# The last layer's first pair of tiles made among the last output products, block sums issued later, and three tiles for the weights' finer sums

## The chip, the cores and the metric

The kernel runs on one core of a Trainium2 chip. Its time is the device time in microseconds (us) of one execution. PE is TensorE (matmuls and transposes), DVE is VectorE, ACT is ScalarE, POOL is GpSimd, and SP is SyncE, whose only work here is to issue DMAs, in order. L1015 is line 1015 of the kernel before.

## The reference, cut to what matters

Four layers act on x, 8 batches of 256 rows by 1024 columns, all in float32. Each layer adds its result, times a gate, to x.

```python
x = x + g0 * autocorrelation(x, ctx)          # through a Fourier transform
x = x + g1 * lora_ffn(norm(x))                # 1024 x 1024 weight with a low-rank part
q, k, v = norm(x) @ wq, ctx @ wk, ctx @ wv    # 32 query heads, 8 key/value groups of 4 heads
x = x + g2 * softmax(mask(rope(q) @ rope(k).T)) @ v @ wo
x = x + g3 * (norm(x) @ w1 + b1)              # the "Fourier" layer; w1 is made on the chip
```

## The kernel before

The batches are done in two passes of four, `p = 0` and `p = 1`. A pass keeps its x as eight tiles of 128 rows by 1024 columns (`xt`), in two blocks `blk` of four tiles. It runs its four layers one after the other: `autocorrelation` with `keys_values` beside it, `lora_ffn`, `attention`, `fourier_ffn`.

The large products are Strassen products: a product of 2 by 2 blocks is made of seven block products (`SEVEN`, in the order 1, 2, 6, 7, 4, 5, 3) on sums of blocks. `left_operands` makes the sums of a left side with four additions or subtractions, and what a product gives is added to x at once by `add_product` (L261 to L275, with the scaled addition `residual`, L381).

**Attention** takes 16 steps (blk, group). A step has four rounds `i`. In each round it issues the `scores` of one batch and head pair (L1142), some of the next step's `queries` (L985), the softmax on ACT and DVE (L1151 to L1165), and the `values` (transposes at L1177, products at L1188). Outputs, the products with `wo`, are generators: `o_gen` is advanced by so many yields at each place (`o_fill`, `fill_from`), so that PE has work while a softmax is under way.

- In pass 0 `outputs` makes the 7 products of one step (L1015, 14 matmul groups of 128x512). `load_wo` brings its seven weight tiles. In the odd steps of block 1 (steps 9, 11, 13 and 15) `finer_weights` also makes, for each of the seven weights, four more half tiles for pass 1: two subtractions on DVE (L931, L932), two on POOL (L933, L934) into the tiles `t67` and `t45`, and a store of each to `wo2_d` (L935, L936). Each of `t67` and `t45` has one buffer, and the generator gives one of the seven per round.
- In pass 1 (`paired`) `outputs_of_two` makes the outputs of two steps at once, with 7 x 7 = 49 products (L1078). POOL makes the finer left operands (`oI`, L1061), DVE combines the quarters (L1086 to L1098), and DVE and POOL add them to x (L1105). The weights come through `stream_wo`: 28 tiles of 4 KB per partition for a pair of steps (four for each of the seven outer products: one in two DMAs of 256 KB, two of 512 KB, one of 256 KB), each issued seven tiles ahead of its use.

When the last step's `values` are issued, the outputs of the last step (p = 0) or the last pair of steps (p = 1) follow with nothing between them. Then `fourier_ffn` begins. It takes its tiles in four pairs. `prepare` takes the norm's statistics of four tiles at once (`norm_stats`: L359, L360), normalises a tile into `xn` (L366, DVE), transposes it on PE (L376, eight transposes per tile) and copies it out of PSUM (L377, ACT). `left` then makes the sums of a pair, and `project` its seven products (L1327, four matmuls each). The next pair is prepared ahead of the products of a pair.

**What decides the order.** The code is written for a tile framework: a scheduler orders each engine's instructions by its own estimates of their times, with the order of the source as priority, and puts in the waits. Buffers come from pools. The two large groups "a" and "b" have seven buffers of 4 KB per partition each (`big_tile`); in a pass, `gq` holds the query weights and later the Fourier weights, and `go` holds the output weights `wo`. A tile that asks for a buffer waits until the earlier one in its slot has no more readers.

Of the kernel before, what the change touches and what calls it, by code (L numbers as in the profile page):

```python
# [11 lines left out]
F32 = mybir.dt.float32  # L12
# [7 lines left out]
P = 128  # L20
# [26 lines left out]
def flamingo_kernel(ctx: ExitStack, tc: tile.TileContext, a: dict, out: bass.AP):  # L47
# [303 lines left out]
    def norm_stats(tiles):  # L351

        n = len(tiles)
        mv = stats.tile([P, TT, 2], F32, tag="mv", name="mv")
        rstd = stats.tile([P, TT], F32, tag="rstd", name="rstd")
        for i, xt in enumerate(tiles):
            st = stats.tile([P, 2, 6], F32, tag="st", name="st")
            for h in range(2):
                nc.vector.bn_stats(st[:, h, :], xt[:, h * HALF : (h + 1) * HALF])  # L359
            nc.vector.bn_aggr(mv[:, i, :], st.rearrange("p a b -> p (a b)"))  # L360
        nc.scalar.activation(rstd[:, :n], mv[:, :n, 1], AF.Sqrt, bias=eps)
        nc.vector.reciprocal(rstd[:, :n], rstd[:, :n])
        return mv, rstd
# [493 lines left out]

    def attention(p, xt, gq, go, keep, norms, xops):  # L860
        with (
            tc.tile_pool(name="at1", bufs=1, reuse_waits="tile") as w1,
            tc.tile_pool(name="at2", bufs=2, reuse_waits="tile") as w2,
# [30 lines left out]
            def load_wo(step):  # L894
                blk, g = step
                if p == 0 and blk == 0:
                    q = [
                        [big_tile(go, [2, HALF], f"wo_{k}{j}") for j in range(2)]
                        for k in range(2)
                    ]  # L900
                    for k, j in ((0, 0), (1, 0), (0, 1), (1, 1)):
                        nc.sync.dma_start(q[k][j], a["wo"][g, k, j])
                    s = [big_tile(go, [2, HALF], f"wo_t{i}") for i in (1, 2, 4)]
                    ops = right_operands(nc.vector, q, *s)
                    for d, r in zip(wo_d[g], (5, 7, 6, 4)):
                        nc.sync.dma_start(d, ops[r])
                else:
                    ops = {}
                    for n, r in enumerate(SEVEN):
                        if g % 2 and n < 2:  # L910
                            ops[r] = w1.tile([P, 2, HALF], F32, tag="wo", name=f"wo_{r}", bufs=2)
                        else:
                            ops[r] = big_tile(go, [2, HALF], f"wo_{r}")
                        nc.sync.dma_start(ops[r], wo_operand(g, r))
                wo[step] = ops
# [5 lines left out]
            def finer_weights(step):  # L921

                blk, g = step
                for n, r in enumerate(SEVEN):
                    w = wo[blk, g - 1][r], wo[step][r]
                    q = [[w[k][:, :, j * S : (j + 1) * S] for j in range(2)] for k in range(2)]
                    t67, t45 = (
                        w1.tile([P, 2, 2, S], F32, tag=f"fine_{i}", name=f"fine_{i}")
                        for i in ("t67", "t45")
                    )  # L930
                    nc.vector.tensor_sub(t45[:, 1], q[0][1], q[0][0])  # L931
                    nc.vector.tensor_sub(t67[:, 1], q[1][1], q[0][1])  # L932
                    nc.gpsimd.tensor_sub(t67[:, 0], q[1][1], t45[:, 1])  # L933
                    nc.gpsimd.tensor_sub(t45[:, 0], t67[:, 0], q[1][0])  # L934
                    nc.sync.dma_start(wo2_d[g // 2][:, n, 0], t67)  # L935
                    nc.sync.dma_start(wo2_d[g // 2][:, n, 1], t45)  # L936
                    yield
# [36 lines left out]
            def half(tag, bufs):  # L974
                return w2.tile([P, 2, S], F32, tag=tag, name=tag, bufs=bufs)
# [50 lines left out]
            def outputs_of_two(blk, qs):  # L1026
# [7 lines left out]
                    ]  # L1034
                    for t in range(2)
                ]
                s1 = [half("oT", 13) for _ in qs]
                for q, s in zip(qs, s1):
                    nc.gpsimd.tensor_add(s, q[1][0], q[1][1])
                    nc.gpsimd.tensor_sub(q[1][0], q[0][0], q[1][0])  # L1040
                at = lambda i, k: [q[i][k] for q in qs]
                ops = {1: at(0, 0), 2: at(0, 1), 6: at(0, 0), 7: at(1, 0), 4: at(1, 1), 5: s1}
                ops[3] = ops[2]

                def quarter(tag, bufs):
# [20 lines left out]
                left, make = finer(SEVEN[0])  # L1066
                for _ in make:
                    pass
                part = None
                for n, r in enumerate(SEVEN):  # L1070
                    coming = finer(SEVEN[n + 1]) if r != SEVEN[-1] else ({}, iter(()))
# [126 lines left out]
            def fill_from(gen, n):  # L1198
                for _ in range(n):
                    next(gen, None)  # L1200
# [26 lines left out]
            def start_outputs():  # L1227
                if paired:
                    got = outputs_of_two(last[0][0][0], [oT for _, oT in last])
                else:  # L1230
                    s = [half(f"oS{j}", 1) for j in (1, 2, 4)]
                    got = outputs(last[0][0], left_operands(nc.gpsimd, last[0][1], *s))
                last.clear()
                return got

            oT = [[None, None], [None, None]]
            for k, step in enumerate(steps):
                follow = k + 1 < len(steps)
                following = {}
                if follow:  # L1240
                    load_kv(steps[k + 1])
                    q_gen = queries(steps[k + 1], following)
                    if k == 0:
                        fill_from(q_gen, 1)
                else:
                    q_gen = nothing
                for i, (n, l) in enumerate(((0, 0), (0, 1), (1, 0), (1, 1))):
                    got = scores(step, l, n, qT)
                    nq = q_fill.get(k, (3, 3, 1, 0))[i]
                    no = o_fill[k][i]  # L1250
                    fill_from(q_gen, nq)
                    mid = min(no, middle)
                    if i > 0:
                        fill_from(o_gen, no - mid)
                    if before is not None:
                        values(*before, lambda: fill_from(o_gen, mid))
                    before = step, l, n, got, oT
                    if i == 0:
                        if len(last) == 1 + paired:
                            o_gen = start_outputs()  # L1260
                            fill_from(o_gen, no)
                        else:
                            fill_from(o_gen, no - mid)
                    if i == 2 and k + 2 < len(steps):
                        if steps[k + 2][1] == 0:
                            blk = steps[k + 2][0]
                            xb = xt[blk * NBT : (blk + 1) * NBT]
                            xops[blk] = query_operands(xb, norms[blk], new_xl, ps_wa, "wa")
                        load_wq(steps[k + 2])
                    if i == 0 and not paired:  # L1270
                        load_wo(step)
                    if i == 0 and p == 0 and step[0] > 0 and step[1] % 2:
                        fine = finer_weights(step)
                    fill_from(fine, 2 if k == end else 1)
                for _ in q_gen:
                    pass
                if not paired or k % 2:
                    for _ in o_gen:
                        pass
                last.append((step, oT))  # L1280
                oT = [[None, None], [None, None]]
                qT = following
            values(*before, lambda: None)
            for _ in start_outputs():
                pass


    def fourier_ffn(p, xt, groups):
        with (
            tc.tile_pool(name="f1c", bufs=1, reuse_waits="tile") as w1,  # L1290
            tc.tile_pool(name="f1", bufs=2, reuse_waits="tile") as w2,
# [5 lines left out]
            bias1 = w1.tile([P, D], F32, name="bias1")  # L1297
            nc.sync.dma_start(bias1, a["b1"].partition_broadcast(P))
            nc.vector.tensor_scalar(bias1, bias1, tg_f[1], None, ALU.mult)
            norms = {}  # L1300

            def prepare(t):
                if t % NBT == 0:
                    norms[t // NBT] = norm_stats(xt[t : t + NBT])
                xn = w2.tile([P, D], F32, tag="xn", name="xn")
                normed(xn, xt[t], *norms[t // NBT], t % NBT)
                xnT = w2.tile([P, KC, P], F32, tag="xnT", name="xnT")
                transposed(xnT, xn, ps_t, "t")
                return xnT
# [33 lines left out]

            pending = None
            for m in range(TT // 2):
                got = left(prepare(m * 2), prepare(m * 2 + 1))
                if pending is not None:
                    project(*pending)
                pending = (m, got)
            project(*pending)  # L1350

    for p in range(NPASS):
# [42 lines left out]
        with tc.tile_pool(name="at_keep", bufs=1, reuse_waits="tile") as kp:  # L1395
# [12 lines left out]
            with tc.tile_pool(name="f0w", bufs=1, reuse_waits="tile") as fw:  # L1408
# [8 lines left out]
                    w0 = stored_weight((gb, ga), lambda r: made.get(r, w0_d[WEIGHTS.index(r)]))  # L1417
                    make_w0 = None
                lora_ffn(xt, w0, make_w0, ag, bl, before_attention)
            attention(p, xt, gb, ga, keep, norms, xops)  # L1420
        fourier_ffn(p, xt, (gb, "xn"))

# [136 lines left out]
```

## Time and profile before

| | |
|---|---|
| three runs | 3377.03, 3388.79, 3388.81 us; median 3388.79 us |
| profiled execution | 3383.27 us |
| its span (first to last instruction) | 3381.5 us |
| mean granted TensorE clock | 0.991 of full speed |
| PE busy | 3278.5 us, 97% of the span |
| DVE busy | 2396.7 us, 71% |
| POOL busy | 1559.5 us, 46% |
| ACT busy | 854.1 us, 25% |
| DMA traffic | 505.56 MB, mean 150 GB/s |

The profile's views used below are these. The page has the busy time of each engine. The groups by line give the number of instructions, their busy time, the mean time of one, and the idle time of the engine ahead of them with what ended it. The list of waits has, by engine and line, how long the engine stood still for which instruction, how often, and the longest. The timeline gives single stretches of one engine in order of time; a bracket says how long the engine was idle before, and what released it. Idle time of an engine that is not the bottleneck costs nothing.

### The profile page before, as it was taken

How to read it: one execution, taken by the hardware profiler on the slowest of the kernel's cores; microseconds unless marked ns; L12 is line 12 of the kernel's file. 1: busy time of each engine (PE TensorE's matmuls, PEld its weight loads, DVE VectorE, ACT ScalarE, POOL GpSimd, SP SyncE). 2: the span in 40 equal slices, each digit the busy share in tenths (PEclk: the TensorE clock that was granted, in tenths of full speed). 3: DMA queues.
4: the chain of work that ended last, by engine and by line, in shares of the span. 5: the costliest groups of instructions: out<-in, count | busy, mean ns of one | idle time of the engine just before them, and what ended most of it. 6: DMA issues, size and time to landing. Idle time of an engine off the chain costs nothing. (4 is left out here: it accounts for less than half of the span.)

```text
span 3381.5 us, 39786 instructions
## 1 busy us (share of the span) xinstructions
PE 3278.5 (97%) x13456; PEld 2411.3 (71%) x13456; DVE 2396.7 (71%) x4549; ACT 854.1 (25%) x2069; POOL 1559.5 (46%) x1445
## 2 busy tenths in 40 slices
PE   8899999999999999999999989999999999999999
PEld 6666546777777766775456667568888888888874
DVE  7787656887777777777648775457777777777773
ACT  1333111322232322223113321113222223222310
POOL 4655212434443555456435552113555554555672
PEclk9999999999999999999999999999999999999999
DMA  7433625333333454555254434043555455555641
GB/s 270 171 116 112 216 98 180 122 135 134 131 128 137 146 181 161 177 204 182 72 191 135 142 106 162 7 156 100 165 168 170 152 170 170 165 164 175 212 147 50
DMA packets 215784, 505.56 MB, mean 150 GB/s; under 512 B 25077, under 2 KB 102901, under 8 KB 215583
## 3 DMA queue, kind: packets, MB, share of 16 engines
q1 hardware_dynamic: 214430, 498.84, 43.8%
q0 software_dynamic: 1152, 4.19, 0.3%
q8 instruction: 107, 1.75, 0.2%
q14 instruction: 95, 0.77, 0.1%
HBM read 394.96 MB, written 108.00 MB: 149 GB/s over the span
## 5 line engine op out<-in xcount | busy, mean ns | idle before, releaser
L728 POOL TENSOR_TENSOR qT<-qT,rope 128x512 f32<-128x512 f32 x128 | 169.6, 1325 | 685.6 <-DVE qT L727 685.6
L985 PE MATMUL ps_q<-xn,wq 128*128 128x256 f32 x1920 | 428.9, 379 | 0.0
L985 PEld LDWEIGHTS ps_q<-xn,wq 128*128 128x128 f32 x1920 | 365.2, 190 | 50.0 <-PE po L688 0.5
L1156 ACT ACTIVATE s<-s,nmx 128x256 f32<-128x256 f32 x512 | 255.9, 500 | 342.5 <-DVE nmx L1153 341.8
L985 PE MATMUL ps_q<-xn_t,wq 128*128 128x256 f32 x1280 | 285.6, 379 | 0.0
L1151 DVE COPY_PREDICATED s<-keep,ps_s 128x512 f32<-128x512 uint8 x256 | 185.3, 729 | 139.9 <-PE ps_s L1142 134.5
L985 PEld LDWEIGHTS ps_q<-xn_t,wq 128*128 128x128 f32 x1280 | 243.5, 190 | 32.8
L381 DVE SCALAR_TENSOR_TENSOR x<-po,tg,x 128x512 f32<-128x512 f32 x248 | 176.8, 743 | 113.1 <-PE po L688 42.2
L1188 PE MATMUL av<-wT,v 128*128 128x256 f32 x1024 | 246.3, 383 | 5.6 <-ACT wT L1183 5.6
L1142 PE MATMUL ps_s<-kT,qT 128*128 128x256 f32 x1024 | 247.6, 379 | 0.0
L1165 DVE TENSOR_SCALAR s<-s,tot 128x256 f32<-128x256 f32 x512 | 236.1, 501 | 7.1
L1188 PEld LDWEIGHTS av<-wT,v 128*128 128x128 f32 x1024 | 192.5, 191 | 60.4 <-issue 22.3
L1183 ACT COPY wT<-pt 128x512 f32<-128x512 f32 x256 | 138.4, 588 | 360.7 <-PE pt L1177 360.4
L1078 PE MATMUL po<-wo,oI 128*128 128x256 f32 x896 | 217.1, 382 | 9.4 <-POOL oI L1061 8.3
L1142 PEld LDWEIGHTS ps_s<-kT,qT 128*128 128x128 f32 x1024 | 192.0, 190 | 25.3 <-issue 0.7
L1015 PE MATMUL po<-wo,oT 128*128 128x512 f32 x448 | 201.5, 592 | 0.0
L1078 PEld LDWEIGHTS po<-wo,oI 128*128 128x128 f32 x896 | 167.6, 190 | 38.0 <-POOL oI L1061 11.8
L1150 POOL MEMSET s<- 128x512 f32 x256 | 128.2, 526 | 129.4 <-PE pt L1177 121.8
L1153 DVE TENSOR_REDUCE nmx<-s 128x2 f32<-128x512 f32 x256 | 174.0, 684 | 7.1
L264 POOL TENSOR_TENSOR x<-x,part 128x512 f32<-128x512 f32 x48 | 68.0, 1417 | 221.0 <-ACT part L263 221.0
L1078 PE MATMUL po<-wo,oT 128*128 128x256 f32 x672 | 167.6, 380 | 2.0 <-DVE co L1093 2.0
L1196 ACT COPY oT<-av 128x512 f32<-128x512 f32 x128 | 74.9, 585 | 370.9 <-PE av L1188 370.9
(296 smaller groups left out, 6502.9 us busy)
## 6 DMA issues: line engine op xcount, KB each, us to landing
wo<-wo_d SPq DMA_DIRECT2D x144, 512.0 KB, 4.7
wq<-in_wq_dram SPq DMA_DIRECT2D x104, 512.0 KB, 3.5
wq<-wq_d SPq DMA_DIRECT2D x96, 512.0 KB, 3.3
wo<-in_wo_dram SPq DMA_DIRECT2D x56, 512.0 KB, 3.6
wo_d<-fine_t SPq DMA_DIRECT2D x56, 512.0 KB, 3.1
wo<-wo_d SPq DMA_DIRECT2D x96, 256.0 KB, 3.4
w<-w_d SPq DMA_DIRECT2D x36, 512.0 KB, 5.3
wo<-in_wo_dram SPq DMA_DIRECT2D x72, 256.0 KB, 3.3
```

Source lines behind the costliest of these rows:

```text
L381: nc.vector.scalar_tensor_tensor(xs, ps, g, xs, ALU.mult, ALU.add)
L728: nc.gpsimd.tensor_add(dst, dst, t)
L985: nc.tensor.matmul(ps[:, l, :], wops[r][:, l, c, :], xo[r][:, c, :], start=(c == 0), stop=(c == KH - 1),)
L1015: nc.tensor.matmul(po, ops[r][:, h, t * P : (t + 1) * P], wops[r][:, h, :], start=(h == 0), stop=(h == 1),)
L1078: nc.tensor.matmul(po, left[r2][:, h, :], w[:, h, :], start=(h == 0), stop=(h == 1))
L1142: nc.tensor.matmul(ps[:, t, :], qT[i, n][:, l, t * P : (t + 1) * P], kT[:, n * S : (n + 1) * S], start=True, stop=True,)
L1151: nc.vector.copy_predicated(s, keep[b], ps)
L1153: nc.vector.tensor_reduce(nmx, s, AX.X, ALU.max, negate=True)
L1156: nc.scalar.activation(s[:, t, :], s[:, t, :], AF.Exp, bias=nmx[:, t : t + 1], accum_out=tot[:, t : t + 1],)
L1165: nc.vector.tensor_scalar(s[:, t, :], s[:, t, :], tot[:, t : t + 1], None, ALU.mult)
L1183: nc.scalar.copy(wT[i], pt)
L1188: nc.tensor.matmul(av[:, i, :], kv[step][1][:, n * 2 + c, :], wT[i][:, c, :], start=(c == 0), stop=(c == 1),)
```

## The change

- `attention` takes a function `ahead`. After the last `values`, the outputs' generator is advanced by 14 of its 49 yields (pass 1) or 2 of its 7 (pass 0), then `ahead` is called, and then the outputs go on. `ahead` is the new `before_fourier`: the norm statistics of x tiles 0 and 1, the two `xn`, their transposes and the left sums of the first pair. Its tiles (two `xn`, two `xnT`, one with two sums, one with the third) come from the group that holds `wo` at that time, and its PSUM tiles from the pool that the softmax transposes use.
- `fourier_ffn` gets this first pair (`first`). The statistics are now taken for two tiles at a time, not four.
- In `outputs_of_two`, the sums for product 5 (`s1`) and the subtraction beside them are issued after the first finer sums.
- In `finer_weights`, `t67` and `t45` come from one tag with three buffers. To pay for it, the separate tag `wo` has one buffer, not two, so that of an odd step's seven `wo` tiles six, not five, lie in the large group. The generator always gives one of its seven per round, also in the last step; what is left over there is issued after the outputs.

```diff
-                        if g % 2 and n < 2:
-                            ops[r] = w1.tile([P, 2, HALF], F32, tag="wo", name=f"wo_{r}", bufs=2)
+                        if g % 2 and n == 0:
+                            ops[r] = w1.tile([P, 2, HALF], F32, tag="wo", name=f"wo_{r}")
...
-                        w1.tile([P, 2, 2, S], F32, tag=f"fine_{i}", name=f"fine_{i}")
+                        w1.tile([P, 2, 2, S], F32, tag="fine", name=f"fine_{i}", bufs=3)
...
-                s1 = [half("oT", 13) for _ in qs]
-                for q, s in zip(qs, s1):
-                    nc.gpsimd.tensor_add(s, q[1][0], q[1][1])
-                    nc.gpsimd.tensor_sub(q[1][0], q[0][0], q[1][0])
...
                 left, make = finer(SEVEN[0])
                 for _ in make:
                     pass
+                ops[5] = s1 = [half("oT", 13) for _ in qs]
+                for q, s in zip(qs, s1):
+                    nc.gpsimd.tensor_add(s, q[1][0], q[1][1])
+                    nc.gpsimd.tensor_sub(q[1][0], q[0][0], q[1][0])
...
-                    fill_from(fine, 2 if k == end else 1)
+                    fill_from(fine, 1)
...
             values(*before, lambda: None)
-            for _ in start_outputs():
+            o_gen = start_outputs()
+            fill_from(o_gen, 14 if paired else 2)
+            ahead(ps_wa, "wa")
+            for _ in o_gen:
                 pass
-    def fourier_ffn(p, xt, groups):
+            for _ in fine:
+                pass
+    def fourier_ffn(p, xt, groups, first):
...
-            norms = {}
-            def prepare(t):
-                if t % NBT == 0:
-                    norms[t // NBT] = norm_stats(xt[t : t + NBT])
+            def prepare(t, norm):
                 xn = w2.tile([P, D], F32, tag="xn", name="xn")
-                normed(xn, xt[t], *norms[t // NBT], t % NBT)
+                normed(xn, xt[t], *norm, t % 2)
...
-                got = left(prepare(m * 2), prepare(m * 2 + 1))
+                if m == 0:
+                    got = first
+                else:
+                    norm = norm_stats(xt[m * 2 : m * 2 + 2])
+                    got = left(*(prepare(m * 2 + i, norm) for i in range(2)))
...
+            def before_fourier(ps_t, tag):
+                norm = norm_stats(xt[:2])
+                tiles = []
+                for t in range(2):
+                    xn = big_tile(ga, [D], "xn")
+                    normed(xn, xt[t], *norm, t)
+                    tiles.append(big_tile(ga, [KC, P], "xnT"))
+                    transposed(tiles[t], xn, ps_t, tag)
+                q = [[s[:, k * KH : (k + 1) * KH, :] for k in range(2)] for s in tiles]
+                both = big_tile(ga, [2, KH, P], "s12")
+                s = both[:, 0], both[:, 1], big_tile(ga, [KH, P], "s4")
+                first.update(left_operands(nc.vector, q, *s))
+            attention(p, xt, gb, ga, keep, norms, xops, before_fourier)
+        fourier_ffn(p, xt, (gb, "xn"), first)
```

More of the change, by code (lines that the diff above doesn't have):

```diff
@@ L851, in query_operands, with attention @@
         return right_operands(nc.vector, q, *s)
-    def attention(p, xt, gq, go, keep, norms, xops):
+    def attention(p, xt, gq, go, keep, norms, xops, ahead):
         with (
@@ L1036, in outputs_of_two @@
                 ]
-                s1 = [half("oT", 13) for _ in qs]
-                for q, s in zip(qs, s1):
-                    nc.gpsimd.tensor_add(s, q[1][0], q[1][1])
-                    nc.gpsimd.tensor_sub(q[1][0], q[0][0], q[1][0])
                 at = lambda i, k: [q[i][k] for q in qs]
-                ops = {1: at(0, 0), 2: at(0, 1), 6: at(0, 0), 7: at(1, 0), 4: at(1, 1), 5: s1}
+                ops = {1: at(0, 0), 2: at(0, 1), 6: at(0, 0), 7: at(1, 0), 4: at(1, 1)}
                 ops[3] = ops[2]
@@ L1419, in flamingo_kernel @@
                 lora_ffn(xt, w0, make_w0, ag, bl, before_attention)
-            attention(p, xt, gb, ga, keep, norms, xops)
-        fourier_ffn(p, xt, (gb, "xn"))
+            first = {}
+            def before_fourier(ps_t, tag):
[12 more added lines that the diff above has]
+        fourier_ffn(p, xt, (gb, "xn"), first)
 def _constants():
```

## The prediction, made before the changed kernel ran

> **What bounds the kernel now.** First the page: who is busy, and with what.
>
> ```profile
> PE 3278.5 (97%) x13456; PEld 2411.3 (71%) x13456; DVE 2396.7 (71%) x4549; ACT 854.1 (25%) x2069; POOL 1559.5 (46%) x1445
> ```
>
> PE is busy for all but 103 us of the span of 3381.5 us. The change leaves PE's work as it is, so it can only take away or add idle time of PE. I therefore went to the list of waits, for those of PE that lie where the change works. The columns are the total, the number of times and the longest, in us.
>
> ```profile
> PE po L1015 <- DVE x L381: 9.4, 6, 3.0
> PE po L1078 <- POOL oI L1061: 8.3, 12, 1.1
> PE pt L376 <- DVE xn L366: 7.9, 5, 3.6
> ...
> PE av L1188 <- ACT wT L1183: 5.6, 3, 2.4
> ...
> PE pt L1177 <- DVE s L1165: 1.8, 1, 1.8
> ```
>
> The wait at L376 is the one that the early pair is about: Fourier transposes standing for the first `xn`. The timeline of PE shows it at the end of pass 0 and of pass 1 (brackets: idle before, and what ended it).
>
> ```profile
> 1626.12 7.03 PE L1015 MATMUL po<-wo,oS 128*128 128x512 f32 x16
> 1635.99 1.38 PE L376 MATMUL pt<-ident,xn 128*128 128x128 f32 x8 [2.84 <-DVE xn L366]
> 1637.58 1.97 PE L376 MATMUL pt<-ident,xn 128*128 128x128 f32 x8 [0.21 <-DVE xn L366]
> ...
> 1641.46 1.97 PE L376 MATMUL pt<-ident,xn 128*128 128x128 f32 x16 [0.76 <-DVE xn L366]
> ```
>
> ```profile
> 3265.84 1.89 PE L1078 MATMUL po<-wo,oI 128*128 128x256 f32 x8
> 3271.30 3.40 PE L376 MATMUL pt<-ident,xn 128*128 128x128 f32 x16 [3.57 <-DVE xn L366]
> ```
>
> The wait at L1015 looks unrelated until DVE is read beside PE, in block 1 of pass 0, where the finer sums are made:
>
> ```profile
> 1216.49 0.69 DVE L932 TENSOR_TENSOR fine_t<-wo,wo 128x512 f32<-128x512 f32 x1 [2.90 <-issue]
> ...
> 1217.62 0.74 DVE L381 SCALAR_TENSOR_TENSOR x<-po,ntg,x 128x512 f32<-128x512 f32 x1
> ```
>
> ```profile
> 1218.42 1.98 PE L1015 MATMUL po<-wo,oS 128*128 128x512 f32 x4 [3.00 <-DVE x L381]
> ```
>
> DVE stood 2.90 us before a finer sum with the addition L381 behind it, and PE stood 3.00 us for that addition. The view of the tile `fine_t` tells why such sums stand: its single buffer is being stored.
>
> ```profile
>   DMA wo_d<-fine_t: 38.2, 19
> ```
>
> PE's gaps of this kind are 3.00 us at 1215.4, 2.63 at 1351.0 and 2.52 at 1486.7, one in each of three odd steps: 8.15 of the 9.4 us.
>
> **The change part by part.** All sums go against the profiled execution, 3383.27 us: its span of 3381.5 and 1.77 around it.
>
> *Three tiles for the finer sums.* With a shared tag of three, the tile for the first DVE sum (`t45`) is free at once, and only one in two sums meets a store that is still out. In the changed kernel's order, the addition L381 that PE waited for stands ahead of the finer sum that waits. What is late next is a finer sum alone, and nobody on PE reads it. So I take all three waits away: -8.2 us. The price: with one tile fewer outside the large group, the second of an odd step's weights is loaded about half a step later, behind PE's release of a slot. The sums start later and six instead of five crowd into the rest of the window. Per sum DVE pays 0.80 + 0.69 us (L931, L932) and POOL 1.28 + 1.27 us, as before. I expect DVE to stand some 2.7 us at the window's end before score masks (L1151); PE has the other queued products of outputs and queries there, so I cost it at nothing. If that cover is gone, it costs the longest wait that is seen at L932, 3.3 us, in three windows, against the 2.7 us a window that vanish: +1.8 us net. The late weight itself takes 3.6 us to land (page, `wo` of 512 KB). PE never waits for `wo` in this block now; uncovered once, it costs +3.6. Part: -9.4 to +5.4, taken -8.2.
>
> *Transition of pass 0.* Taken out: 2.84 + 0.21 + 0.76 = 3.8 us. Added: both early `xn` have one slot in the large group. So the second cannot be written before PE has transposed the first; behind that wait DVE's queue stands, and ahead of it an addition L381 that itself waits for POOL. Its bounds are the sum alone, 2.6 us (two `xn` of 0.8 and one addition of 0.74, with queueing), and 3.9 with the POOL step of 1.27 (128x512) also bare; taken 3.3. The output's own left sums on POOL come later: 1.1 us. Three of the last step's seven finer sums now run after the outputs, and one, 2 x 0.69 = 1.4 us of DVE, I put in front of an addition PE needs: 1.3. On the other side, with one and not two sums a round in the last step, the waits 1.39 (`av`) and 1.78 (L1177) there may go. Not counted, since ACT, not a finer sum, released the first. The loads of the next pass's `ctx` are issued later too on SP, behind the slots of the early pair; keys and values start some 90 us after the transition begins, which I take as cover enough. Sum 3.3 + 1.1 + 1.3 - 3.8 = +1.9, ends -7.0 (3.8 + 3.2 gained) and +5.
>
> *Transition of pass 1.* Taken out: 3.57. Added, first, two short waits for the early `xn`, again on one slot: 0.8 us each less the products between; 1.4 in all, ends 0 and 2. Second, the weights' stream. The early pair holds four of the seven slots until its Fourier products are done, so the last 14 weight tiles go through three slots. SP issues a load only when PE has finished the tile three before, and everything behind it on SP waits as well. How long a load takes:
>
> ```profile
> wo<-in_wo_dram SPq DMA_DIRECT2D x56, 512.0 KB, 3.6
> ```
>
> ```profile
> wo<-wo_d SPq DMA_DIRECT2D x7, 512.0 KB, 4.8
> ...
> wo<-wo_d SPq DMA_DIRECT2D x10, 512.0 KB, 6.4
> ```
>
> The first is the page's median; the others are those of 3190 to 3226 us and 3225 to 3275 us, the latter with seven tiles in flight, where most of it is queueing. PE uses four tiles in 6.04 us (28 matmuls of 0.216), 1.51 each. With three slots a cycle is issue 0.3 + landing L + use 1.5, for three tiles. At 3.6 that is 5.4 us, 1.80 a tile, +0.29 for each of the 11 tiles after the first three: +3.2 us. At 4.8 it is +7.6, at 6.4 +13.4. With only three in flight I take 3.6, the row for loads that don't queue.
>
> [...]
>
> Third, the end of the outputs. The last additions to x still come about as late, and the second pair now needs its `xn` there: some 3.6 us (the wait of today) less about 1.7 us of first-pair products (four matmuls of 0.43) that the order puts there, +1.9, ends 0 and 2.5. Sum -3.6 + 1.4 + 3.2 + 1.9 = +2.9, ends -3.6 and +8.5.
>
> *The rest.* Statistics of two tiles add two table loads on ACT (1.28 us each in the timeline at 3284.7) where ACT is 25% busy: nothing. The sums for product 5 hardly move, since the scheduler already had the first finer sums ahead of them: nothing, at most one wait of 1.1 us at L1078.
>
> Total: -8.2 + 1.9 + 2.9 = -3.4, so 3379.9 in this execution's terms. The median of the runs lies 5.5 us above the profiled execution, the lowest 6.2 below. Between 3379.9 and 3385.4 I put 3382.
>
> **The rivals.** *The stream ends on the slower side.* If three slots land like the loaded window, 6.4 us, the stream costs 13.4 and the total is +6.8: 3390 us. The sum turns positive where the stream costs over 6.6 us, at L = 4.5. For it: 4.8 and 6.4 stand in the very stretch. Against: those loads queue behind six others. With the fine waits not gone either, it is +15, 3398.
>
> *The waits form again.* The sixth sum crowds the window, and PE stands as before, only later. Then the first part is worth nothing: +4.8, 3388. For it: DVE is busy for 33.05 of 46 us in the window at 1184, and the stores still take 3.1 us. Against: L381 is now ahead.
>
> *All is gained.* If the stream keeps up (L under 2.7) and the early pair meets no wait, it is 9.4 + 7.0 + 3.6 = -20: 3363 us. Only a single 256 KB load comes near such an L (3.3), and both early tiles share a slot, so it is the least supported.
>
> **How the numbers follow.** Forecast case 0.50, the slower stream 0.20, waits again 0.15, all or most gained 0.15. About 0.5%, 17 us, is what a measurement of this kernel tells from no change. Beyond it on the fast side lie 0.11 of the last case and 0.02 of the first; on the slow side 0.06 of the stream's, 0.03 of the third. So 0.13 faster, 0.78 same, 0.09 slower. The ends of the parts add up to -20 and +19; with the runs' own spread of some 6 us either way, but not all ends at once, 8 in 10 lie within 3366 and 3400.
>
> **What would show it.** Right: no wait of 2.5 us or more at L1015 near 1215, 1351 and 1486; the wait at L376 with its 3.57 split into smaller ones; `wo` landing near 3.6 us in the last 20 us of attention, and PE idle for DMA `wo` there, 3 us in all, which the list of waits does not have now. Wrong: over 7 us of such idle time; new waits for fine or masks in the three windows; or PE's busy time itself changing.

## The result and the profile after

| | before | after |
|---|---|---|
| median (14 runs each) | 3386.47 us | 3387.45 us |
| lowest to highest | 3377.03 to 3390.31 | 3378.8 to 3391.76 |
| span of the profiled execution | 3381.5 us | 3386.4 us |
| PE busy | 3278.5 us | 3283.1 us |

The ratio is 0.9999, with a 95% interval from 0.9991 to 1.0007: no change that can be measured. The forecast was 3.4 us faster, a ratio of 0.9990. Of the waits that the change was to remove, those at L1015 are gone and those at L376 fell from 7.9 to 4.6 us; others stand in their place. The list of waits of PE, after:

```profile
PE av L1190 <- ACT wT L1185: 13.7, 6, 4.2
...
PE pt L376 <- DVE xn L366: 4.6, 4, 2.0
PE po L1080 <- DMA wo<-wo_d: 3.6, 5, 0.9
...
PE ps_q L987 <- DVE x L381: 2.7, 3, 0.9
```

No row for L1017 (L1015 before) behind DVE is left: the 9.4 us are gone, as forecast (8.2 of them). The wait for ACT `wT` has grown from 5.6 to 13.7 us, and there are five waits for weights that did not exist.

To see where time goes at this size, one needs a finer ruler than the total, which differs by 13 us between runs of one kernel. I used starts of instructions that both kernels have: the copies of `oT` (L1196, 128 in all) on ACT, and PE's first `ps_k` of pass 1. *Block 1* is from the 33rd to the 64th copy, *transition* from there to that `ps_k`, *end* from the 128th copy to the end of the span, all in us.

| kernel | block 1 | transition | end |
|---|---|---|---|
| before | 489.87 | 133.05 | 155.55 |
| after | 491.27 | 131.03 | 159.29 |
| e1 finer sums alone | 491.07 | 132.40 | 153.92 |
| e2 early pair alone | 489.41 | 131.28 | 159.36 |
| e3 after, pair at 35 | 489.24 | 131.08 | 153.60 |
| e4 after, sums on POOL | 501.72 | 132.67 | 159.34 |
| e5 e3, two sums at the end | 493.53 | 129.62 | 153.50 |
| e6 e3, finer sums as before | 486.74 | 131.70 | 153.50 |
| e7 e3, sums on DVE | 477.64 | 135.32 | 153.61 |
| e8 before, one `wo` tile | 487.96 | 136.92 | 155.46 |
| e9 as e7 | 477.63 | 135.42 | 153.62 |
| e10 e7, two sums at the end | 481.20 | 130.68 | 153.61 |
| e11 before, sums on DVE | 476.31 | 133.68 | 155.57 |
| e12 e6, sums on DVE | 476.13 | 132.14 | 153.48 |

The three differences of after add up to +1.4 - 2.0 + 3.7 = +3.1 us. PE's idle time between its first and its last instruction is 91.8 us before and 92.1 after. Each row is one trace. Traces whose code is the same in block 1 show what such a row can tell: before, e2 and e6 have 489.9, 489.4 and 486.7 us, after and e3 491.3 and 489.2. So +1.4 in block 1 is not told from nothing. The 12 to 14 us that e7, e9, e11 and e12 gain there are.

**Block 1.** In steps 9 to 14 (37th to 61st copy) after is 3.3 us shorter, which e6 is too, with the finer sums of before. In step 15 (to the 64th) after is 5.1 us longer: 31.4 against 26.3, where e2 and e6 have 26.4 and 26.5. The view of the tile `fine_t`, after, gives the idle time of DVE and POOL ahead of the sums:

```profile
  DMA wo_d<-fine_t: 36.6, 19
  DMA wo<-wo_d: 24.9, 10
  DMA wo<-in_wo_dram: 8.5, 8
```

Three tiles took away almost nothing of the standing for stores (38.2 before), and the sums now also wait for weights: 33.4 us against 4.5 before. What then waits for DVE has changed. Timelines of DVE and PE, after:

```profile
1229.95 0.69 DVE L934 TENSOR_TENSOR fine_t<-wo,wo 128x512 f32<-128x512 f32 x1 [2.24 <-DMA wo_d<-fine_t]
1230.56 0.68 DVE L1155 TENSOR_REDUCE nmx<-s 128x2 f32<-128x512 f32 x1
```

```profile
1234.75 1.99 PE L1190 MATMUL av<-wT,v 128*128 128x256 f32 x8 [1.87 <-ACT wT L1185]
```

The finer sum waits for a store with the softmax's maximum (L1155) behind it. ACT's exponentials wait for that maximum, the copy `wT` stands behind them on ACT, and PE runs out of products before it. ACT at that place:

```profile
1231.28 0.51 ACT L1158 ACTIVATE s<-s,nmx 128x256 f32<-128x256 f32 x1 [12.36 <-DVE nmx L1155]
...
1234.11 1.07 ACT L1185 COPY wT<-pt 128x512 f32<-128x512 f32 x2
```

It is the same fault as before, with a reduction in the place of the addition. It comes in each of the three windows (1.87, 1.92 and 1.45 us), each time with a wait of 0.9 for x at L987: 2.80, 2.84 and 2.35 us where 3.00, 2.63 and 2.52 stood before. The last step has it once more, and longer:

```profile
1588.12 1.18 DVE L934 TENSOR_TENSOR fine_t<-wo,wo 128x512 f32<-128x512 f32 x1 [3.07 <-DMA wo_d<-fine_t]
```

```profile
1593.46 3.78 PE L1190 MATMUL av<-wT,v 128*128 128x256 f32 x8 [4.17 <-ACT wT L1185]
```

The eight products take 3.78 us here and 1.99 above; the granted clock is 0.50 from 1592.4 to 1599.0 us and 1.00 from 1230 to 1237. The last section comes back to that.

**End of pass 1.** The stream through three slots shows as forecast:

```profile
3258.45 1.97 PE L1080 MATMUL po<-wo,oT 128*128 128x256 f32 x8 [0.77 <-DMA wo<-wo_d]
3261.87 1.97 PE L1080 MATMUL po<-wo,oI 128*128 128x256 f32 x8 [0.59 <-DMA wo<-wo_d]
```

The issues of DMAs between 3236 and 3282 us give the landings, in their last column:

```profile
wo<-wo_d SPq DMA_DIRECT2D x8, 512.0 KB, 4.9
wo<-wo_d SPq DMA_DIRECT2D x9, 256.0 KB, 3.3
```

### The profile page after: what moved, and what is told of

It reads as the page before. It is cut to its first block, busy times and chain, and to the rows that moved or that the text cites. A ratio compares the mean times of both kernels' runs of the same rounds, so it can differ in the third digit from the quotient of the medians.

```text
span 3386.4 us, 39800 instructions
## 1 busy us (share of the span) xinstructions
PE 3283.1 (97%) x13456; PEld 2409.3 (71%) x13456; DVE 2413.7 (71%) x4553; ACT 858.2 (25%) x2075; POOL 1570.9 (46%) x1445
## 5 line engine op out<-in xcount | busy, mean ns | idle before, releaser
L987 PE MATMUL ps_q<-xn,wq 128*128 128x256 f32 x1920 | 429.2, 379 | 2.7 <-DVE x L381 2.7
L987 PEld LDWEIGHTS ps_q<-xn,wq 128*128 128x128 f32 x1920 | 364.5, 190 | 54.3 <-DVE x L381 3.9
L987 PE MATMUL ps_q<-xn_t,wq 128*128 128x256 f32 x1280 | 285.6, 379 | 0.0
L987 PEld LDWEIGHTS ps_q<-xn_t,wq 128*128 128x128 f32 x1280 | 243.2, 190 | 33.1
L381 DVE SCALAR_TENSOR_TENSOR x<-po,tg,x 128x512 f32<-128x512 f32 x248 | 178.3, 744 | 121.5 <-PE po L1332 43.5
L1190 PE MATMUL av<-wT,v 128*128 128x256 f32 x1024 | 248.5, 386 | 13.7 <-ACT wT L1185 13.7
L1167 DVE TENSOR_SCALAR s<-s,tot 128x256 f32<-128x256 f32 x512 | 245.7, 520 | 7.1
L1144 PEld LDWEIGHTS ps_s<-kT,qT 128*128 128x128 f32 x1024 | 193.6, 192 | 26.3 <-issue 0.7
L1017 PE MATMUL po<-wo,oT 128*128 128x512 f32 x448 | 201.8, 593 | 0.0
L1155 DVE TENSOR_REDUCE nmx<-s 128x2 f32<-128x512 f32 x256 | 174.1, 683 | 6.9
```

The source lines that it names most:

```text
L381: nc.vector.scalar_tensor_tensor(xs, ps, g, xs, ALU.mult, ALU.add)
L987: nc.tensor.matmul(ps[:, l, :], wops[r][:, l, c, :], xo[r][:, c, :], start=(c == 0), stop=(c == KH - 1),)
L1017: nc.tensor.matmul(po, ops[r][:, h, t * P : (t + 1) * P], wops[r][:, h, :], start=(h == 0), stop=(h == 1),)
L1144: nc.tensor.matmul(ps[:, t, :], qT[i, n][:, l, t * P : (t + 1) * P], kT[:, n * S : (n + 1) * S], start=True, stop=True,)
L1155: nc.vector.tensor_reduce(nmx, s, AX.X, ALU.max, negate=True)
L1167: nc.vector.tensor_scalar(s[:, t, :], s[:, t, :], tot[:, t : t + 1], None, ALU.mult)
```

## The experiments

**e1: the finer sums alone.** To the kernel before:

```diff
-                        if g % 2 and n < 2:
-                            ops[r] = w1.tile([P, 2, HALF], F32, tag="wo", name=f"wo_{r}", bufs=2)
+                        if g % 2 and n == 0:
+                            ops[r] = w1.tile([P, 2, HALF], F32, tag="wo", name=f"wo_{r}")
...
-                        w1.tile([P, 2, 2, S], F32, tag=f"fine_{i}", name=f"fine_{i}")
+                        w1.tile([P, 2, 2, S], F32, tag="fine", name=f"fine_{i}", bufs=3)
...
-                    fill_from(fine, 2 if k == end else 1)
+                    fill_from(fine, 1)
...
+            for _ in fine:
+                pass
```

> The kernel before with only the finer-sum edit (three shared tiles, one separate wo tile, one sum per round, the rest after the outputs). If the waits of block 1 were turned into softmax waits by this edit alone: from the 37th to the 61st copy of oT (L1196) 394.2 us as in the changed kernel, against 397.5 before; from the 61st to the 64th 31.4 against 26.3; PE waits for ACT wT about 13 us in all, no wait of 2.5 us at L1015; the last stretch of pass 1 (from the 128th copy of oT to the end) 155.5 as before. If instead the early pair's tiles cause the last step's loss, that step stays at 26.3 and the span is 3 us shorter than before.

From the 37th to the 61st copy it took 392.3 us, then 33.1: the last step's loss is there without the early pair, and somewhat more than forecast. PE's waits in block 1 were 9.3 us for `wT` and none at L1015. So the finer sums alone turn one wait into the other. The end is 153.9 us, not the 155.5 forecast; the last section has the reason.

**e2: the early pair alone.**

To the changed kernel, e1's diff taken back, with single buffers and two separate `wo` tiles again.

> The changed kernel with the finer sums as before (early pair and moved block sums stay). If the parts are independent: waits of 3.0, 2.6 and 2.5 us at L1015 are back, 397.5 us from the 37th to the 61st copy of oT and 26.3 to the 64th; from there to the first keys of pass 1 131.0 or less against 133.05 before; the end of pass 1 159.3 against 155.5 with 3.6 us of PE waiting for DMA wo in five places. If the changed last step came from the early pair, it shows here as 31.4.

Block 1 is that of before (397.0 and 26.4 us, with the waits at L1017 back), the transition 131.3, the end 159.4. As far as these traces tell, the parts are independent, and the early pair costs in pass 1 what it gains in pass 0 and more.

**e3: the early pair later in pass 1.**

```diff
-            fill_from(o_gen, 14 if paired else 2)
+            fill_from(o_gen, 35 if paired else 2)
```

> The changed kernel with the early pair put after 35 instead of 14 of the 49 yields in pass 1. If three slots for the weights cost the 3.7 us: PE no longer waits for DMA wo there (0 to 0.5 us), the stretch from the 128th copy of oT to the end falls from 159.3 to 155 or less. If the two waits for xn cost it, they stay (2.1 us) and the stretch stays over 157. A rival: the second xn now comes so late that its wait grows to 3.5 us, as in the kernel before, and the stretch is 155.5 or more.

The end falls by 5.7 us to 153.6. By the 35th yield nearly all weights have been issued. The list of waits of PE from 3227 to 3290 us in e3:

```profile
PE po L1080 <- issue: 1.5, 1, 1.5
PE pt L376 <- DVE xn L366: 1.2, 2, 0.6
```

No weight is waited for. The waits for `xn` are smaller too (1.2 against 2.1), so the rival falls. The three slots were the cost: 3.6 of the 5.7 us are the waits for weights themselves.

**e4: all finer sums on POOL.**

```diff
-                    nc.vector.tensor_sub(t45[:, 1], q[0][1], q[0][0])
-                    nc.vector.tensor_sub(t67[:, 1], q[1][1], q[0][1])
+                    nc.gpsimd.tensor_sub(t45[:, 1], q[0][1], q[0][0])
+                    nc.gpsimd.tensor_sub(t67[:, 1], q[1][1], q[0][1])
```

> The changed kernel with all four finer sums on POOL, none on DVE. If what costs is DVE's queue standing behind a sum that waits for a store or a weight: the waits of PE for ACT wT in block 1 of pass 0 (10.7 us in the changed kernel, 1589 us included) go to under 3, and the stretch from the 37th to the 64th copy of oT falls from 425.6 to 416. If the softmax then stands behind POOL's queue instead (the memset ahead of the mask, the rotation of queries), the waits come back at the same places and the stretch is 425 or more. POOL has 28 x 2 x 1.27 = 71 us more work in 490.

Block 1 got 10.5 us longer than in after, to 501.7, and the stretch 436.1. The second theory holds in part: in block 1 DVE stood 27.4 us for POOL's memset ahead of the mask, against 3.7 in after. But DVE itself became slow too, in an instruction that has nothing to do with the sums. DVE and POOL in e4:

```profile
1584.88 6.59 DVE L1167 TENSOR_SCALAR s<-s,tot 128x256 f32<-128x256 f32 x2
1591.40 0.15 DVE L1165 RECIPROCAL tot<-tot 128x2 f32<-128x2 f32 x1
1591.59 0.62 DVE L1167 TENSOR_SCALAR s<-s,tot 128x256 f32<-128x256 f32 x2
```

```profile
1583.16 1.31 POOL L935 TENSOR_TENSOR fine_t<-wo,fine_t 128x512 f32<-128x512 f32 x1
1584.40 1.32 POOL L933 TENSOR_TENSOR fine_t<-wo 128x512 f32<-128x512 f32 x1
1585.65 1.29 POOL L936 TENSOR_TENSOR fine_t<-fine_t,wo 128x512 f32<-128x512 f32 x1
1586.87 1.29 POOL L269 TENSOR_TENSOR x<-x,part 128x512 f32<-128x512 f32 x1
1588.10 1.29 POOL L934 TENSOR_TENSOR fine_t<-wo,wo 128x512 f32<-128x512 f32 x1
```

Two scalings took 0.62 us where POOL was idle, and 6.59 us where POOL had one sum after another. POOL's sums took 1.3 us each there, against 1.28 and 1.27 in the kernel before. PE's waits in block 1 came to 18.5 us: 7.4 for `qT` (L250, DVE), 6.0 for `wT` and 5.1 for x (L381, DVE). Neither theory had DVE as the slow one. How much of these waits is the memset and how much the slow scaling, no run separates.

**e5: two sums a round at the end.** To e3:

```diff
-                    fill_from(fine, 1)
+                    fill_from(fine, 2 if k == end else 1)
```

> The changed kernel with the early pair after 35 yields in pass 1, and two finer sums per round again in the last step of pass 0. If the last step's loss comes from spreading its seven sums over more rounds than before: from the 61st to the 64th copy of oT 26 us (31.6 with one per round), PE's wait of 4.2 us for ACT wT near 1589 is gone, and the steps before stay at 392.0 from the 37th to the 61st. Then the kernel is 0.2 to 0.3% faster than before, 3376 to 3380 against 3387. If it comes from the wo tile that loads later, the step stays at 30 or more and the gain is 0.1% or less.

Ratio 0.9995 (0.9986 to 1.0004). The last step took 33.1 us, not 26: its loss does not come from the number of sums per round. The steps before took 394.8, not 392.0.

**e6: e3 with the finer sums as before**, that is with e1's diff taken back.

> The same with the finer sums wholly as before; only the early pair (after 35 yields in pass 1) and the moved block sums are left. If the parts add up: block 1 of pass 0 as before (397.5 and 26.3 us, with the waits of 3.0, 2.6 and 2.5 at L1015), the transition of pass 0 131 against 133, the end of pass 1 153.6 against 155.5: 4 us or 0.1% faster than before.

Ratio 0.9992 (0.9983 to 1.0001). The waits at L1017 were back (3.0, 2.5 and 2.5 us), the end was 153.5, the stretches of block 1 394.2 (forecast 397.5) and 26.5. The sign is as forecast, but the interval still holds 1.

**e7: e3 with all finer sums on DVE**, after e4 had shown DVE held up by POOL.

```diff
-                    nc.gpsimd.tensor_sub(t67[:, 0], q[1][1], t45[:, 1])
-                    nc.gpsimd.tensor_sub(t45[:, 0], t67[:, 0], q[1][0])
+                    nc.vector.tensor_sub(t67[:, 0], q[1][1], t45[:, 1])
+                    nc.vector.tensor_sub(t45[:, 0], t67[:, 0], q[1][0])
```

> The changed kernel with the early pair after 35 yields and all four finer sums on DVE, none on POOL. If DVE's softmax scaling (L1167) is held up by POOL's sums running beside it: its mean falls from 520 to under 500 ns, the softmax waits of PE in block 1 (ACT wT) fall below 5 us, and block 1 takes under 488 us (489.2 in the run with one edit less). If DVE has no room for 28 x 2 x 0.69 = 39 us more, or if its standing for stores is what counts, the waits stay or grow and block 1 takes 490 or more.

Block 1 fell to 477.6 us, 11.6 less than e3, PE's idle time in it from 13.3 to 4.2. The mean of L1167 over the whole run went from 522 ns in e3 to 477. The transition rose to 135.3: sums left over from the last step stand on DVE ahead of the early `xn` (PE waits 3.8 us at L376). e10 tests that.

**e8: one separate `wo` tile.** To the kernel before:

```diff
-                        if g % 2 and n < 2:
-                            ops[r] = w1.tile([P, 2, HALF], F32, tag="wo", name=f"wo_{r}", bufs=2)
+                        if g % 2 and n == 0:
+                            ops[r] = w1.tile([P, 2, HALF], F32, tag="wo", name=f"wo_{r}")
```

> The kernel before with one separate wo tile in place of two, and nothing else; the finer sums keep one buffer each. If the late second weight is what makes DVE stand for weights: fine_t's waits for DMA wo rise from 4.5 us to 25 or more, and block 1 is 1 to 5 us longer than before (489.9). If the weights' waits come from the shared tag instead, they stay under 6 and block 1 at 490.

A miss of the first theory. The waits for weights came to 8.2 us, not 25, and block 1 got no longer. But its last step took 29.6 us (26.3 before) and the transition 136.9. So, as far as one trace shows it, part of the last step's loss belongs to the late weight; the rest comes only together with the shared tag.

**e9 to e12**, on one chip. e9 is e7 again; e10 is e7 with e5's diff; e11 is the kernel before with e7's diff and nothing else; e12 is e6 with e7's diff.

> The kernel of the look before last (early pair after 35 yields, all four finer sums on DVE), now timed against the kernel before. If its stages are what they were: block 1 of pass 0 477.6 against 489.9 us, the transition 135.3 against 133.05, the end of pass 1 153.6 against 155.5: 11.9 us, 0.35% faster, ratio 0.9955 to 0.9975. If the single look was a lucky one, the ratio's interval holds 1.

> The same with two finer sums a round in the last step of pass 0, so that fewer are left for DVE ahead of the early xn. If the longer transition (135.3 against 131.1 us) comes from those sums: it falls to 131, PE's wait of 3.8 us for xn at L376 to 2, and the last step stays at 26.9: 0.45% faster than before. If crowding the last step costs as much, as it did with sums on POOL (33.1 against 31.6), the last step rises by as much as the transition falls.

> The kernel before with its two POOL sums put on DVE, and no other edit: single buffers, two separate wo tiles, no early pair. If it is POOL beside DVE that costs, by the longer chain to the store and by holding up DVE: the mean of L1165 falls from 501 to under 480 ns, the waits for stores from 38 to under 15 us, the waits of 3.0, 2.6 and 2.5 at L1015 to under 1 each, and block 1 takes under 482 us against 489.9; 0.2% or more faster. If three tiles are needed for that, the three waits stay over 1.5 us each and block 1 is over 486.

> The edit of the run before with the early pair after 35 yields: finer sums on DVE in single buffers, two separate wo tiles, two sums a round at the end. If the parts add up, it has that kernel's block 1, a transition of 131 to 133 and an end of pass 1 of 153.6: 2 to 4 us faster than that kernel. If the early xn meets the finer sums on DVE, the transition rises to 135 and the gain goes.

| kernel | ratio to before | 95% interval | median us (before 3385.1) |
|---|---|---|---|
| e9 | 0.9971 | 0.9959 to 0.9983 | 3374.24 |
| e10 | 0.9959 | 0.9944 to 0.9974 | 3371.19 |
| e11 | 0.9966 | 0.9953 to 0.9980 | 3374.90 |
| e12 | 0.9953 | 0.9940 to 0.9966 | 3368.87 |

e9 came within its forecast. e11 is the kernel before with two words changed: 13.6 us less in block 1, with single buffers, and the mean of L1165 466 ns. Its waits for stores are 23.8 us, more than the 15 that I expected, but PE's wait at L1015 is gone and 3.1 us of softmax waits are left in block 1. So three tiles were not needed. e12 adds the late early pair: 2.1 us less at the end and 1.5 in the transition, and the expected rise to 135 did not come. It is 0.47% faster than the kernel before. Its interval overlaps that of e11, so what the early pair adds is seen in the stages alone; and of the 2.1 us at the end the pair itself gives some 0.4, since e1, without it, ended in 153.9. In e10 the transition fell as expected (130.7), the last step rose to 29.8, and the sum is a little better than e9; their intervals overlap.

## Why the prediction was right, and where its steps were not

**The total.** "0.78 same" was the case that came, and the range held the time. The sum behind it did not: the three stages give +3.1 us where it had -3.4, so it missed by 6.5 us and in its sign. A range of 34 us and a resolution of 17 us hide that: the forecast held by their width, not by its mechanism. What came is the rival "the waits form again", whose total was 3388, and with it a sign that the prediction itself had named for being wrong: new waits in the three windows.

**The finer sums, -8.2.** This step failed. Its first half held: L381 stands ahead of the waiting sum, and the three waits at L1015 are gone. The second half, "PE has the other queued products ... so I cost it at nothing", did not. The 2.7 us of DVE that I saw ahead of the masks came, as a wait of 2.2 ahead of a maximum, and PE had 1.87 us too little queued. In block 1 after the softmax waits come to 13.4 us of PE's time together with L987; before, L1015 and softmax 12.6. In these two traces the part is +1.4; shown is that nothing was gained, not the sign. This was the rival "the waits form again", which had 0.15. What I did not see at all was the last step, where I had thought that waits might go: 5.1 us came. One reading ahead of the sum rests on more than its row: the wait of 2.90 us is put down to `issue`, not to a store. But SP issued the store of that tile at 1213.39, and 3.1 us later, the profile page's median for such a store, is the 1216.49 at which the sum starts.

**The transition of pass 0, +1.9.** Wrong in sign, small: -2.0. The second `xn` on the first one's slot did make PE wait:

```profile
1617.92 1.88 PE L1017 MATMUL po<-wo,oS 128*128 128x512 f32 x4
1621.83 1.06 PE L376 MATMUL pt<-ident,xn 128*128 128x128 f32 x8 [2.02 <-DVE xn L366]
```

That is 2.02 us, where I took 3.3. The 1.1 for POOL's sums and the 1.3 for a finer sum did not appear: PE had products there.

**The end of pass 1, +2.9.** Right in sign and near in size: +3.7 (+5.4 against e1, where no half clock followed the last gap). The stream cost 3.6 us, and 0.7 more that the list puts down to issue; I had 3.2. That the term fits is luck, for its inputs were wrong. I took the landing of another load, `wo<-in_wo_dram`; the profile page's row for the stream's own, `wo<-wo_d`, had 4.7, and 4.9 came, which by my formula makes 8.0. Against that, 9 of the 17 loads in the view above have 256 KB and landed in 3.3 us, where I took every tile for one load of 512 KB. The Fourier products that the order puts between the outputs must have hidden a part too; no run shows how much. The `xn` waits were 2.1 (taken 1.4); the wait at the very end, +1.9, did not come. That the stream would cost was right.

**The cause, as the runs show it.** I read "a DVE sum waits for its buffer" and followed the buffer. The mean time of the softmax scaling in block 1 (groups by line, 1120 to 1600 us) tells the rest. Before, after, e4 and e11:

```profile
L1165 DVE TENSOR_SCALAR s<-s,tot 128x256 f32<-128x256 f32 x116 | 63.4, 587 | 1.3
```

```profile
L1167 DVE TENSOR_SCALAR s<-s,tot 128x256 f32<-128x256 f32 x116 | 72.4, 665 | 1.3
```

```profile
L1167 DVE TENSOR_SCALAR s<-s,tot 128x256 f32<-128x256 f32 x114 | 98.0, 900 | 1.7
```

```profile
L1165 DVE TENSOR_SCALAR s<-s,tot 128x256 f32<-128x256 f32 x120 | 48.7, 447 | 1.0
```

With two sums on POOL 587 and 665 ns, with four 900, with none 447. It was held up while POOL summed: in the whole trace of the kernel before, the 374 scalings during which POOL did nothing took 349 ns on the average, none over 356; the 118 that ran beside a `TENSOR_TENSOR` of POOL and no memset took 906, from 336 to 1475.

Moving the sums to DVE also cuts the chain from weight to store, from 1.27 to 0.69 us a sum. And POOL's additions to x no longer stand behind its finer sums: before, DVE waited 10.1 us for them ahead of L931 in block 1, in e11 not at all. How the 13.6 us divide between the three stays open: no run changed one without the others. On PE's side they are 9.5 us less idle time in block 1 (12.7 to 3.3), and the two stretches at half clock that followed waits before are not there. But e6 has none either, with two sums on POOL, so that part is not shown to be the change's.

## What to carry to other kernels

More buffers for a tile that waits gained nothing here (block 1 took 491.3 us in after, 489.9 before): a maximum that the softmax needed stood behind the waiting sum, and the sums waited 33.4 us for weights. Look at what comes next in the queue, and at what feeds the buffers' inputs. When two engines share a job, read each one's mean time in the stage with and without the other: work moved from POOL (busy 266 of 480 us) to a DVE that was already busier (349) was worth 13.6 us of block 1, and 0.34% of the time. Before an early preparation takes slots from a stream, count how many loads are still to be issued.

## What the runs showed of the hardware that I had not expected

**POOL's sums held DVE up.** In e4 a pair of scalings took 0.62 us where POOL was idle and 6.59 us where POOL summed (both shown above). Five POOL instructions of 1.3 us, from 1584.40 to 1590.61, got through while that one pair stood.

**An idle gap cost more than its length in some places.** The 16 transposes after the gap of 3.57 us at the end of pass 1 took 3.40 us before (shown with the prediction). In e1, after a gap of 3.61:

```profile
3268.93 1.94 PE L376 MATMUL pt<-ident,xn 128*128 128x128 f32 x16 [3.61 <-DVE xn L366]
```

Before, the granted clock from 3260 to 3275 us is 0.89, in e1 1.00. In e8 (3275 to 3290) and e11 (3260 to 3275), after gaps of 3.6 us, it is 0.89 again. In those three the end is 155.5, in e1 153.9. In block 1 the clock is 0.50 for 3.41 us or twice that at a time: before, 3.41 us from 1353.3 and from 1489.8; after, 3.41 from 1370.4 and 6.83 from 1592.3. Shorter gaps than 3.6 us are followed by half clock too. In the kernel before:

```profile
1489.25 3.25 PE L1015 MATMUL po<-wo,oS 128*128 128x512 f32 x4 [2.52 <-DVE x L381]
```

The same four products took 1.98 us after the gap of 3.00 us (shown with the prediction). In after, the clock is 0.50 for 3.41 us from 1623.0, behind the gap of 2.02. The nine gaps at the end of pass 1 after, the longest 1.7 us, were followed by none. What decides, these traces do not show.

So a wait counted for more in places than the list of waits says. In e4, block 1 has 5.3 us more idle time than in after and is 10.5 longer; 23.9 us of it ran at half clock against 10.2. The spread between traces of the same code goes with it too: before has 6.8 us of half clock in block 1, e2 3.4, e6 none. And PE's busy time, 4.6 us more in after for the same 13456 instructions, need not be more work: the mean granted clock was 0.990 against 0.991.
